# Own emission times for the last three groups, a direct last layer-2 product, and the first input in four loads

## The chip, the cores and the metric

The kernel runs on one core of one Trainium2 chip. The metric is the device time of one execution in microseconds (us). Every execution told of here was in the fast state, so nothing in this document compares runs of different states. The time of an execution is 1.7 to 2.9 us, mostly 1.8, longer than the span from the first to the last instruction; positions below are counted inside that span.

## The reference

Four graph layers work on 128 graphs of 128 nodes and 512 features, all in float32. They share one adjacency matrix `adj` of 128x128, and each is followed by a residual addition and a layer normalisation. Cut to what matters:

```python
x = ln(x + einsum('nm,bmd->bnd', adj, x) @ w0 + bias)                 # layer 0
q, k, v = x @ wq.T, x @ wk.T, x @ wv.T                                # layer 1
rel = adj.T * (q @ k^T);  rel = rel / norm(rel, axis=2)
x = ln(x + rel @ v)
h = x @ w2;  s1 = h @ a1;  s2 = h @ a2                                # layer 2
e = leaky_relu(s1[:, :, None] + s2[:, None, :]) * adj
x = ln(x + elu(softmax(e) @ h + beta * h))
A = adj @ x;  pre = A[:, :, None, :] + (C - A)[:, :, :, None]         # layer 3, C = A + b
x = ln(x + max(relu(pre), axis=-1))
```

## The kernel before

The graphs go through in 32 groups of four, numbered 0 to 31. Matrix products are done by TensorE, the rest by VectorE, ScalarE and GpSimd. Every operation is emitted with a time of its own. All are sorted by that time, and each engine then does its share strictly in the order that comes out; only the order matters, not the value of a time. One table serves all groups, each 28 steps behind the one before it, so that four groups in different layers overlap in the steady state:

```python
def emit(at, f, *args):
    pieces.append((at, lambda: f(*args)))
...
    # layer 2 of one group, t = 28 * g
    emit(t + 61.6, spread)          # p_s: s2 spread over the rows (TensorE)
    emit(t + 62.0, leaky)           # e (VectorE), then times adj (GpSimd)
    ...
    emit(t + 65.8, divide)          # softmax division of all four graphs (GpSimd)
    emit(t + 68.6, turn_att)        # p_eT: transposes
    each(t + 71.5, 1.0, gather)     # p_z, one graph each; ScalarE copies to zT
    left_factors(t + 75.3, s, "zT", "s_yz", f"z_{g}", 0)   # block sums s_z (GpSimd)
    product(t + 77, f"z_{g}", by_rows, s, "2", ...)        # r_z: seven block products
...
for g in range(NG):
    for layer in (layer0, layer1, layer2, layer3):
        layer(g, 28.0 * g)
for _, f in sorted(pieces, key=lambda p: p[0]):
    f()
```

The four large products of a group (called r_y, r_m, r_v and r_z in the profile) are done for four graphs together, in two by two blocks, with seven block products in place of eight. The price is sums of blocks: GpSimd makes four sums of the left factor (s_y, s_x, s_z), VectorE makes those of the weights once (t_m, t_v), and the results come out of PSUM through ScalarE copies and VectorE additions:

```python
def out(i):
    p, dst = r[REGION[i]], c(*BLOCK[i])
    if fresh and i in (1, 6, 5, 4):
        act.copy(dst, p)
    else:
        dve.tensor_tensor(dst, p, dst, ALU.add)
for n, i in enumerate(ORDER):
    emit(at + n, step, i)
    emit(at + n + 0.72, out, i)
```

The start loads the adjacency matrix and the first group's x as one megabyte on the SP queue, and w0, the bias, wk and w2 on the ScalarE queue. ScalarE then copies the transposed adjacency matrix `adjT` that the first product needs:

```python
def load(g):
    x1[g] = data.tile([P, G, D], FP, tag="x1", name=f"x1_{g}", bufs=3)
    nc.sync.dma_start(x1[g], x[g * G : (g + 1) * G].rearrange("b n d -> n b d"))
load(0)
nc.scalar.dma_start(w0_sb, w0.rearrange("(k p) f -> p k f", p=P))
nc.scalar.dma_start(bias_sb, on_all(bias0, D))
...
act.copy(adjT, pt[:, :P])
```

Names that come up again, in the order of a group's life: p_y (adjacency times x), r_y, p_xT (transposes), r_m (x times the product of wq and wk; tT is its result in SBUF), p_rel, r_v, p_o (attention output, then the residual x of layer 1), scr and d (the dot products for s1 and s2), p_s, e, p_eT, p_z, r_z, c (the layer-2 product), x3 (its residual), p_a (layer 3), mx and top (its maximum), st and mv (statistics).

## Time and profile before

| | before |
|---|---|
| time, median of 3 runs | 2324.65 us (2324.57 to 2328.68) |
| profiled span | 2324.9 us |
| TensorE busy | 2255.3 us, 97% |
| waits of TensorE in the first 130 us | 16.5 us |
| A: start of the last group's first r_m | 2187.26 us |
| from A to the end | 137.6 us |

TensorE is the bound in the middle. What can be had lies at the two ends, where no other group is there to fill the gaps. The lines for this are in the prediction. Later sections use one more stretch of the kernel before, the timeline of TensorE where it waits for the dot products d of group 0. The columns are start, us, engine, line, operation, output and inputs, sizes and count, then the idle time before it and what ended it:

```profile
118.91 0.62 PE L26 MATMUL p_s<-ident,d 128*128 128x128 f32 x4 [2.10 <-DVE d L26]
119.42 2.85 PE L26 MATMUL r_m<-xT,t_m 128*128 128x256 f32 x8
122.06 4.49 PE L26 MATMUL r_y<-w_sb,yT 128*128 128x256 f32 x16
```

After an idle time of 2.10 us, eight matmuls of r_m took 2.85 us and sixteen of r_y 4.49 us. Their usual times are 2.0 and 3.62.

### The profile page before, as it was taken

The numbers are of one execution on the slowest core, as the hardware profiler recorded it, in microseconds if no ns is written. First come the engines' busy times: TensorE is split into PE (matmuls) and PEld (weight loads), VectorE is DVE, ScalarE is ACT, GpSimd is POOL, SyncE is SP. The second block draws the span as 40 slices with busy tenths as digits, with TensorE's granted clock in tenths as the row PEclk, the third lists the DMA queues.
The fourth block names the chain that finished last, engine by engine and source line by source line (L and its number), as shares of the span: only waits on it lengthen the run. The fifth ranks groups of instructions, "written<-read, shape, count | busy, mean of one in ns | idle before, by whom it ended". The sixth has DMA issues, their size and how long they took to land.

```text
span 2324.9 us, 31209 instructions
## 1 busy us (share of the span) xinstructions
PE 2255.3 (97%) x11833; PEld 1922.6 (83%) x11833; DVE 1573.4 (68%) x3300; ACT 1007.8 (43%) x1804; POOL 960.9 (41%) x774
## 2 busy tenths in 40 slices
PE   7999999999999999999999999999999999999964
PEld 5888888888888888888888888888888888888753
DVE  3756776666776666776666776666776666777664
ACT  2224444444444444444445444444444444444434
POOL 3434444434444433444433444433444434444221
PEclk9999999999999999999999999999999999999987
DMA  4000011110011010011110011110011110010000
GB/s 159 19 16 9 32 37 37 37 37 10 28 37 37 37 37 14 24 37 37 37 37 19 19 37 37 37 37 19 19 37 37 37 37 19 19 37 19 19 18 36
DMA packets 38837, 75.20 MB, mean 32 GB/s; under 512 B 2976, under 2 KB 3104, under 8 KB 38688
## 3 DMA queue, kind: packets, MB, share of 16 engines
q1 hardware_dynamic: 36960, 69.81, 8.4%
q10 hardware_dynamic: 1728, 3.41, 0.4%
q8 instruction: 93, 1.52, 0.3%
q14 instruction: 56, 0.46, 0.1%
HBM read 39.65 MB, written 33.55 MB: 31 GB/s over the span
## 4 chain that ended last, share of the span: by engine, by line
PE 94%; DVE 3%; issue 1%; ACT 1%; POOL 1%; DMA 0%; POOLq 0%; ACTq 0%; SPq 0%; DVEq 0%
PE r_y L26 16%; PE r_v L26 16%; PE r_z L26 16%; PE r_m L26 16%; PE p_z L26 5%; PE p_a L26 5%; PE p_rel L26 5%; PE p_y L26 5%; PE p_o L26 5%; PE p_xT L26 2%; PE p_n L26 1%; DVE x L26 1%; DVE st L26 1%; PE p_eT L26 1%; PE p_m L26 1%
## 5 line engine op out<-in xcount | busy, mean ns | idle before, releaser
L26 ACT ACTIVATE x<-x,nmean,rstd 128x512 f32<-128x512 f32 x512 | 385.8, 808 | 134.3 <-DVE nmean L26 134.3
L26 DVE BATCH_NORM_STATS2 st<-x 128x6 f32<-128x512 f32 x512 | 352.5, 688 | 80.4 <-ACT x L26 71.7
L26 POOL TENSOR_TENSOR rstd<-ve,mhalf 128x4 f32<-128x4 f32 x128 | 141.8, 1108 | 258.2 <-DVE ve L26 255.1
L26 POOL TENSOR_TENSOR x<-x,bias_sb 128x512 f32<-128x512 f32 x128 | 175.3, 1371 | 136.5 <-PE p_y L26 136.5
L26 DVE SCALAR_TENSOR_TENSOR scr<-x,wa 128x512 f32<-128x512 f32 x256 | 212.7, 882 | 0.0
L26 ACT ACTIVATE x<-x,top 128x512 f32<-128x512 f32 x128 | 92.4, 722 | 265.5 <-DVE top L26 203.6
L26 DVE TENSOR_TENSOR x<-r_y,x 128x512 f32<-128x512 f32 x224 | 152.9, 683 | 59.1 <-PE r_y L26 56.0
L26 DVE TENSOR_TENSOR v<-r_v,v 128x512 f32<-128x512 f32 x96 | 65.9, 686 | 184.1 <-PE r_v L26 180.4
L26 POOL TENSOR_TENSOR s_x<-xT 128x512 f32<-128x512 f32 x64 | 81.9, 1279 | 235.8 <-ACT xT L26 235.8
L26 ACT COPY yT<-p_y 128x512 f32<-128x512 f32 x128 | 75.1, 587 | 219.9 <-PE p_y L26 219.9
L26 DVE SCALAR_TENSOR_TENSOR x<-p_o,rn,x 128x512 f32<-128x512 f32 x128 | 96.0, 750 | 101.3 <-PE p_o L26 98.3
L26 DVE SCALAR_TENSOR_TENSOR x<-m,x 128x512 f32<-128x512 f32 x128 | 113.7, 888 | 63.7 <-ACT m L26 52.7
L26 ACT COPY c<-r_z 128x512 f32<-128x512 f32 x128 | 74.9, 585 | 186.3 <-PE r_z L26 110.6
L26 PEld LDWEIGHTS p_y<-adjT,x 128*128 128x128 f32 x1024 | 136.7, 195 | 15.1 <-issue 8.7
L26 PE MATMUL p_a<-x,adjT 128*128 128x512 f32 x256 | 136.5, 618 | 13.0 <-ACT x L26 13.0
L26 PE MATMUL p_y<-adjT,x 128*128 128x128 f32 x1024 | 137.3, 279 | 8.5 <-DMA x<-in_x_dram 8.5
L26 PEld LDWEIGHTS p_z<-eT,x 128*128 128x128 f32 x1024 | 135.6, 193 | 8.5 <-issue 2.1
L26 PEld LDWEIGHTS p_rel<-tT,xT 128*128 128x128 f32 x1024 | 134.0, 192 | 6.5
L26 PE MATMUL p_z<-eT,x 128*128 128x128 f32 x1024 | 135.9, 276 | 0.0
L26 PE MATMUL p_rel<-tT,xT 128*128 128x128 f32 x1024 | 134.5, 275 | 0.0
L26 POOL TENSOR_TENSOR s_z<-zT 128x512 f32<-128x512 f32 x32 | 40.5, 1266 | 226.0 <-ACT zT L26 226.0
L26 PE MATMUL p_o<-v,rel 128*128 128x512 f32 x256 | 130.8, 593 | 0.0
(117 smaller groups left out, 5084.3 us busy)
## 6 DMA issues: line engine op xcount, KB each, us to landing
x<-in_x_dram SPq DMA_DIRECT2D x32, 1024.0 KB, 5.2
out_dram<-x SPq DMA_DIRECT2D x128, 256.0 KB, 2.0
w_sb<-in_L_gnn_weight_dram ACTq DMA_DIRECT2D x1, 1024.0 KB, 5.6
wq_sb<-in_L_gnn_Wq_dram SPq DMA_DIRECT2D x1, 1024.0 KB, 15.8
wk_sb<-in_L_gnn_Wk_dram ACTq DMA_DIRECT2D x1, 1024.0 KB, 12.2
wv_sb<-in_L_gnn_Wv_dram SPq DMA_DIRECT2D x1, 1024.0 KB, 18.9
w_sb<-in_L_gnn_W_dram ACTq DMA_DIRECT2D x1, 1024.0 KB, 17.1
a_sb<-in_L_gnn_a_dram SPq DMA_DIRECT2D x1, 512.0 KB, 16.1
```

What stands on the lines that cost most here:

```text
L26: return lambda *args, **kw: self.tc.keep_in_program_order(op(*args, **kw))
```

## The change

It has four parts.

1. The first group's x comes in four loads of 256 KB, one per graph, so that the first product can start on the first quarter. wk moves from the ScalarE queue to the SP queue.
2. Behind the product of wq and wk (p_m) the order is new: the transposes of wv come first, then the second group's four p_y. The four bias additions of the second group move ahead with its p_y.
3. The last three groups get rows of their own in the table, with times in units of one r step of 2.48 us, counted from A. The last group's normalisations of layers 2 and 3, its softmax division (there on VectorE in place of GpSimd) and its stores go graph by graph.
4. The last group's layer-2 product is done graph by graph, with four matmuls of 128x512 each, straight from w2. It needs no block sums, and it is read from PSUM without a copy. For this w2's block stays unchanged and its difference goes into a tile of its own.

The core of the diff, long parts cut:

```diff
+        if g == 0:
+            for b in range(G):
+                nc.sync.dma_start(x1[g][:, b, :], x[b])
+        else:
+            nc.sync.dma_start(x1[g], x[g * G : (g + 1) * G].rearrange("b n d -> n b d"))
...
-    nc.scalar.dma_start(wk_sb, wk.rearrange("(k p) f -> p k f", p=P))
+    nc.sync.dma_start(wk_sb, wk.rearrange("(k p) f -> p k f", p=P))
...
+    FIRST = {1: dict(y=row(-9.5, 0.3), bias=row(-9.2, 0.3))}
+    LAST = {
+        NG - 3: dict(exp=[0.8, 1.5, 2.2, 11.0], elu=[9.7, 12.3, 14.6, 17.2], ...),
+        NG - 2: dict(
+            scale=[5.6], apply1=row(24.3, 0.8), spread=[6.9], leaky=[7.4], ...
+            gather=row(36.7, 0.9), z_sums=row(39.95, 1.3),
+            z_w=[40.0, 41.8, 43.5, 45.2, 47.0, 49.4, 51.1], ...
+            elu=row(56.9, 2.3), norm2=[66.1], ...),
+        NG - 1: dict(
+            m=[0.0, 1.73, 3.46, 5.2, 7.4, 9.1, 10.8], scores=row(12.7, 0.9), ...
+            exps=row(53.2, 0.6), divide=row(53.9, 0.6), ...
+            gather=[55.2, 56.1, 60.5, 65.0], z_w=[57.0, 61.5, 66.0, 69.5], ...
+            store=[89.2, 91.0, 91.9, 92.8]),
+    }
...
+        def direct(b):
+            s["c", b] = psum.tile([P, D], FP, tag="r", name=f"c_{g}_{b}")
+            for k in range(K):
+                pe.matmul(s["c", b], s["zT"][:, k, b * P : (b + 1) * P],
+                          w2_sb[:, k, :], start=(k == 0), stop=(k == K - 1))
...
+        if g < NG - 1:
+            left_factors(t["z_sums"], s, "zT", "s_yz", f"z_{g}", 0)
+            product(t["z_w"], f"z_{g}", by_rows, s, "2", rows_of(lambda: s["c"]), True, begin)
+        else:
+            each(t["z_w"], direct)
...
-    each(26.0, 0.3, prepare_v)
+    each(row(18.0, 0.1), prepare_v)
```

## The prediction

> **What bounds the kernel now.** I read the page's busy times first, then the waits of TensorE, then the timeline of TensorE with its gaps, then ten-microsecond windows of the end.
>
> ```profile
> PE 2255.3 (97%) x11833; PEld 1922.6 (83%) x11833; DVE 1573.4 (68%) x3300; ACT 1007.8 (43%) x1804; POOL 960.9 (41%) x774
> ```
>
> TensorE is busy for 97% of 2324.9 us. The waits of TensorE between 140 and 2190 us are an empty list, so nothing but less matrix work could speed up the middle, and this change keeps that work. What can be had is 2324.9 - 2255.3 = 69.6 us of idle TensorE, plus matmuls that run at a lowered clock. The waits of TensorE in the first 130 us:
>
> ```profile
> PE p_y L26 <- DMA x<-in_x_dram: 8.5, 1, 8.5
> PE p_adjT L26 <- DMA adj_sb<-in_adj_dram: 3.3, 1, 3.3
> PE p_s L26 <- DVE d L26: 2.1, 1, 2.1
> PE r_m L26 <- DVE tT L26: 1.0, 1, 1.0
> PE p_xT L26 <- ACT x L26: 1.0, 1, 1.0
> PE r_y L26 <- POOL s_y L26: 0.6, 1, 0.6
> ```
>
> Columns: who waited for whom, us in total, times, longest. That is 16.5 us, half of it for x of the first group. The timeline of TensorE at the end (start, us, what, idle before it and its releaser):
>
> ```profile
> 2187.26 3.62 PE L26 MATMUL r_m<-xT,m_qk 128*128 128x256 f32 x16
> ...
> 2209.19 1.11 PE L26 MATMUL p_eT<-ident,e 128*128 128x128 f32 x4 [5.67 <-POOL e L26]
> 2210.10 3.22 PE L26 MATMUL r_v<-wvT,xT 128*128 128x256 f32 x8
> ...
> 2251.51 1.11 PE L26 MATMUL p_s<-ident,d 128*128 128x128 f32 x4 [4.42 <-DVE d L26]
> 2266.01 1.12 PE L26 MATMUL p_eT<-ident,e 128*128 128x128 f32 x4 [13.38 <-POOL e L26]
> ...
> 2304.78 5.46 PE L26 MATMUL p_a<-x,adjT 128*128 128x512 f32 x8 [12.15 <-ACT x L26]
> ```
>
> From the last group's first product (2187.26, called A) to the end there are 137.6 us. TensorE idles 5.67 + 4.42 + 13.38 + 12.15 us in four gaps, 2.7 us in three small ones, and about 14.7 us after its last matmul. There is no other group's work to fill the gaps, because all groups follow one table of times made for the steady state.
>
> **The Trainium skill.** "TensorE: Matmul & The Clock Gate", section "What's actually happening", says that the array's clock halves after an idle window of some 3.4 us and recovers after about as long a busy one. The trace agrees: r_v after the 5.67 us gap took 3.22 us, against 1.89 us elsewhere, and the granted clock of 2200 to 2210 us is 0.80. So each gap of two or more microseconds costs about 1.9 us more (0.5 on p_eT, 1.3 on r_v). "DMA: Bandwidth & Descriptors", section "Queues, rings and completion order", says that the SP and ACT queues share the same 16 engines and that completion is not first in, first out per issuing engine. The trace agrees as far as it goes: w0, issued at 0.74, landed at 6.3, and x, issued at 1.18 and as large, only at 12.06.
>
> **Part 1, first x in four loads.** PE needs the first quarter (256 KB), not all of x. In the trace the equally large bias load, issued at 1.23, landed at 8.5; I expect the first quarter by 7 to 8. But the ACT queue of the new kernel makes its third load (w2) wait for w0 (6.3 before), and in program order that load stands before ACT's table load and the copy adjT, which TensorE needs too. So adjT comes at 6.3 + 0.5 (issue) + 1.28 (table load) + 0.27 (copy) = 8.4, against 4.8. The first matmul moves from 12.2 to about 8.5: 3.7 us gained. It starts slow, 1.7 us per graph as before, and the remaining quarters (estimate: by 11.5) keep ahead. Everything up to the end of p_m at 45.34 was one chain behind it, with 0.63 us of gap, so it moves along to 41.6. wk now goes on the SP queue; it lands at about 18 (by bytes: 4.5 MB at the 345 GB/s that the first 22 us moved), before its use at 28.
>
> **Part 2, order behind p_m.** Now come the transposes of wv, then the second group's four p_y, then the four xT, then r_m alone. PE's work up to r_y of group 1 is unchanged: 1.74 + 3.5 + 1.74 + 7 x 1.73 = 19.1 us; before it took 22.3. In the new order p_y must wait for the bank that wvT frees, behind ACT's three x normalisations (2.12) and the copies 0.58 and 0.5: 1.3 us of idle, and the last copies of xT add a little. I get 20.6, a gain of 1.7. The wait of 2.1 for d stays, since VectorE is busy from 83 to 118 with the same list. Together the steady state starts 3.7 + 1.7 = 5.4 us earlier. Its 30 groups keep their order but for one instruction's operand (a weight block in a copy of its own).
>
> **Part 3, the end.** New positions count from A. One r step takes 1.73, p_a 0.86 per graph, p_z 0.87, p_rel 0.22 per matmul. VectorE takes 2.32 per graph of the x3 chain (x, x, st, mv), 1.6 per residual with st, 0.61 per scr, 0.92 per mx with top, 0.83 per st with mv. ACT takes 0.73 per 512-wide activation, POOL 1.27 per block sum and 1.0 per power. I laid these by hand along each engine's new order.
> - p_s of group 30 moves one step forward (6.9), so e is ready at 8.9, its exponentials at 14.5. TensorE has r_v 1 to do (17.0 to 18.8) while POOL divides (done at 17.1). The 5.67 gap and its slow clock go; p_rel waits about 1 us for tT, as ACT's exponentials now stand before that copy.
> - r_v with the p_a of group 29 ends at 33.8. Here VectorE and ACT lag: st of group 29's first graph waits for ACT (28.9 to 29.7), and ACT's copy of v comes at 36. The p_o and p_z share four PSUM banks, which the residuals free 1.6 us apart: p_o and p_z end at 44.7 instead of the table's 40, some 4 us lost.
> - r_z of group 30 waits once for POOL's sums (0.8), and runs to 58.2 with p_s of group 31 inside at 54.3. VectorE loses 1.5 us waiting for rstd. The 4.42 gap goes.
> - e of group 31: 55.1 to 56.4 on VectorE, 57.7 POOL, 58.5 the maximum, first exponential 59.7, division by graph on VectorE 60.1, p_z at 61.0. Of the 13.38 gap 2.8 is left, and the slow clock with it (1.9).
> - From 61.0: four p_z (3.5), 16 direct matmuls of 128x512 (13.9 by p_m, 1.8 more than the 12.1 of seven r_z), transposes 0.3, slow clock 1.9: c ends at 80.6. The old way would wait for sums and copies (0.70 and 1.06 in the trace), and needs all c before the first x3; that was the 12.15 gap.
> - VectorE becomes the bound: x3 of group 30 from 62 to 71, x3 of group 31 to 85.9, between them mx, then four st, mx, st by graph: 100.6 for the last nmean. One ACT apply 0.8 (four took 2.93), and from the last apply to the end 3.05 as before: 104.6.
>
> So the end falls from 137.6 to 104.6: 33.0 us. Sum 5.4 + 33.0 = 38.4; 2324.65 - 38.4 = 2286.
>
> **Rivals.** First, the table comes true: its last store stands at 92.8, with 0.8 and 3.05 behind it 96.7, 41 us gained at the end and 46 in all: 2278, just at 2%. For it: TensorE's work behind A is only about 77 us. Against it: VectorE's list alone takes 29.6 of the 37 us before p_z ends, and its in-order waits for ACT are not in the table. Second, VectorE's and ACT's order blocks more than I laid (each waits for the other in turn at p_a, mx, top, st, as the trace shows with 0.85 us before st each time), and two more gaps bring the slow clock: some 8 to 10 us lost, 2295. Third, w0 shares its bandwidth with the quarters of x and lands late, so adjT holds TensorE and the start gains only 1 to 2 us: 2289. Fourth, the start's gain is hidden because weights come late: wk at 18 against 28 speaks against it.
>
> **Range and chances.** The middle is fixed work, runs agree within 0.2% (2324.57 to 2328.68), and only about 85 us of known gaps can move. The start may be 2 us off, the hand-laid end 6 us: 2279 to 2294. More than 2% needs 2278.2 or less, which only the first rival gives: 0.09. Slower has nothing for it.
>
> **What would show it.** Right: p_y near 8.5 held by adjT rather than x; no gap above 2 us between A and A + 55; one gap of 2 to 4 us before p_z of the last group; VectorE busy almost without pause in the last 40 us; A to the end near 105. Wrong: A later than 2184, TensorE waiting longer than 2 us in the p_o and p_z stretch or for s_z, ACT rather than VectorE at the head of the last chain, or TensorE waits appearing in the steady groups.

## The result, and the profile after

| | before | after |
|---|---|---|
| time, median | 2326.66 us (4 runs, 2324.57 to 2328.75) | 2291.24 us (4 runs, 2290.3 to 2292.32) |
| profiled span | 2324.9 us | 2288.5 us |
| mean granted TensorE clock | 0.988 | 0.996 |
| first p_y starts | 12.20 | 8.45 |
| p_m starts | 31.60 | 27.40 |
| first r_y of group 1 starts | 67.65 | 64.26 |
| A | 2187.26 | 2182.83 |
| from A to the end | 137.6 | 105.7 |

The ratio of the times is 0.9848, with a 95% interval of 0.9831 to 0.9865. Ratios here are the mean time of one kernel's fast runs over that of the other's of the same rounds, so they are not quite the ratio of the medians quoted. The change is 1.5% faster, which is "within 2%". All outputs were correct.

The busy times of the kernel after:

```profile
PE 2250.7 (98%) x11809; PEld 1914.8 (84%) x11809; DVE 1577.0 (69%) x3319; ACT 1005.3 (44%) x1800; POOL 959.2 (42%) x775
```

TensorE's busy time fell by only 4.6 us. The other 31.8 of the 36.4 us by which the span fell were idle TensorE.

**The start.** These are the waits of TensorE in the first 130 us (who waited for whom, us in total, times, longest):

```profile
PE p_y L26 <- ACT adjT L26: 4.7, 1, 4.7
...
```

The wait of 8.5 us for x is gone. The first product now waits 4.7 us for adjT. Two new waits have come, 1.75 us for the block sums s_x and 1.52 for wvT, the transposed wv (both in the timeline below); a third, of 0.43 for x in r_y, comes after the wait for d. The waits for tT and for x in p_xT, 1.0 us each, are gone. The timeline of ScalarE says why adjT is late:

```profile
6.42 0.39 ACTq L114 DMA_DIRECT2D w_sb<-in_L_gnn_W_dram  x1
6.84 1.28 ACT L26 ACT_TABLE_LOAD   x1 [6.84 <-DMA w_sb<-in_L_gnn_weight_dram]
8.13 0.27 ACT L26 COPY adjT<-p_adjT 128x128 f32<-128x128 f32 x1
```

The third load of the ScalarE queue was held until w0 had landed, and the table load and the copy stand behind it. The hold came with the four loads. In one_load (below), where only these are undone, the same load goes out at 1.78 us and adjT is ready at 4.09. Why four loads bring it, no run shows. Behind p_m the timeline of TensorE and that of GpSimd read:

```profile
41.13 1.91 PE L26 MATMUL p_wv<-ident,wv_sb 128*128 128x128 f32 x16
44.56 3.84 PE L26 MATMUL p_y<-adjT,x 128*128 128x128 f32 x32 [1.52 <-ACT wvT L26]
...
50.05 3.72 PE L26 MATMUL r_m<-xT,m_qk 128*128 128x256 f32 x16
55.52 1.99 PE L26 MATMUL r_m<-s_x,t_m 128*128 128x256 f32 x8 [1.75 <-POOL s_x L26]
```
```profile
45.80 6.33 POOL L26 TENSOR_TENSOR x<-x,bias_sb 128x512 f32<-128x512 f32 x4 [13.00 <-PE p_y L26]
52.09 1.71 POOL L26 TENSOR_TENSOR s_x<-xT 128x512 f32<-128x512 f32 x1
```

GpSimd first did the four bias additions of the second group, for 6.33 us, and only then the sum that TensorE needed. And at the wait for d, which stood at 118.91 before:

```profile
115.51 0.62 PE L26 MATMUL p_s<-ident,d 128*128 128x128 f32 x4 [2.10 <-DVE d L26]
116.02 2.00 PE L26 MATMUL r_m<-xT,t_m 128*128 128x256 f32 x8
117.85 3.62 PE L26 MATMUL r_y<-w_sb,yT 128*128 128x256 f32 x16
```

The idle time is the same 2.10 us, but the matmuls behind it ran at full speed this time: 5.62 us in place of 7.34. That was luck, as shown below.

**The end.** The waits of TensorE from 2150 us on:

```profile
PE p_eT L26 <- DVE rs L26: 2.2, 2, 1.7
PE p_a L26 <- DVE mx L26: 1.8, 1, 1.8
PE p_a L26 <- ACT x L26: 1.7, 1, 1.7
...
```

Nothing is longer than 1.8 us; before, the list held 38.2 us, now it holds 10.2. The timeline of TensorE in the second half of that stretch:

```profile
2231.26 3.72 PE L26 MATMUL r_z<-t,s_z 128*128 128x256 f32 x16 [1.67 <-POOL s_z L26]
2236.10 1.97 PE L26 MATMUL r_z<-t,zT 128*128 128x256 f32 x8 [1.12 <-ACT c L26]
2237.91 0.65 PE L26 MATMUL p_s<-ident,d 128*128 128x128 f32 x4
...
2243.74 0.30 PE L26 MATMUL p_eT<-ident,e 128*128 128x128 f32 x1 [1.72 <-DVE rs L26]
...
2244.65 1.74 PE L26 MATMUL p_z<-eT,x 128*128 128x128 f32 x8
```

The first p_z took 1.74 us, in place of 1.05: the clock was down again, after idle times of 1.72 and 0.47 us. Beside the wait for s_z, the timeline of VectorE shows the dot products of the last group:

```profile
2229.40 0.68 DVE L26 SCALAR_TENSOR_TENSOR scr<-x,wa 128x512 f32<-128x512 f32 x1
...
2230.01 1.74 DVE L26 SCALAR_TENSOR_TENSOR scr<-x,wa 128x512 f32<-128x512 f32 x1
```

The same instruction on the same sizes took 0.68 us, and 1.74 us while GpSimd was making block sums. From 2246.93 to the end of its last instruction at 2283.66, the idle times that VectorE shows are 1.55, 0.17 and 0.65 us. So it is busy almost without pause; whether it alone sets the pace is tested below (x3_early).

### The profile page after: what moved, and what is told of

Its sections match the earlier page's. It is cut to its first block, busy times and chain, and to the rows that moved or that the text cites. A ratio compares the mean times of both kernels' runs of the same rounds, so it can differ in the third digit from the quotient of the medians.

```text
span 2288.5 us, 31182 instructions
## 1 busy us (share of the span) xinstructions
PE 2250.7 (98%) x11809; PEld 1914.8 (84%) x11809; DVE 1577.0 (69%) x3319; ACT 1005.3 (44%) x1800; POOL 959.2 (42%) x775
## 3 DMA queue, kind: packets, MB, share of 16 engines
q8 instruction: 93, 1.52, 0.3%
## 4 chain that ended last, share of the span: by engine, by line
PE 94%; DVE 4%; POOL 1%; ACT 1%; issue 1%; DMA 0%; ACTq 0%; DVEq 0%; POOLq 0%
PE r_y L26 17%; PE r_v L26 16%; PE r_m L26 16%; PE r_z L26 16%; PE p_z L26 5%; PE p_rel L26 5%; PE p_o L26 5%; PE p_a L26 5%; PE p_y L26 5%; PE p_xT L26 2%; DVE x L26 1%; PE p_n L26 1%; DVE st L26 1%; PE p_eT L26 1%; PE p_m L26 1%; PE p_s L26 1%
## 5 line engine op out<-in xcount | busy, mean ns | idle before, releaser
L26 POOL TENSOR_TENSOR rstd<-ve,mhalf 128x4 f32<-128x4 f32 (+1 forms) x134 | 144.5, 1078 | 245.3 <-DVE ve L26 241.3
## 6 DMA issues: line engine op xcount, KB each, us to landing
w_sb<-in_L_gnn_W_dram ACTq DMA_DIRECT2D x1, 1024.0 KB, 10.2
```

Of the source, the lines that this page charges most:

```text
L26: return lambda *args, **kw: self.tc.keep_in_program_order(op(*args, **kw))
```

## The experiments

All kernels gave correct results and all runs were fast. The edits are against the kernel after; the name of each run stands behind "Measured". "Before" is the median of the kernel before on the same chip in the same rounds. The kernel after was not run again, and the kernel before moved between 2326.58 and 2328.05 from batch to batch. So a difference from the 2291.24 of the kernel after compares medians of different rounds, and only the interval of start_only is clear of its interval (0.9831 to 0.9865). For differences of a few us positions in the traces are the better guide, but each trace is one execution.

### The start alone, and the end alone

The two halves of the change, each by itself:

```diff
# start_only
-    LAST = { ... }
+    LAST = {}
-        if g < NG - 1:
+        if g < NG:
# end_only
-        if g == 0:  (four loads)
+        nc.sync.dma_start(x1[g], x[g * G : (g + 1) * G].rearrange("b n d -> n b d"))
-    nc.sync.dma_start(wk_sb, ...)
+    nc.scalar.dma_start(wk_sb, ...)
-    FIRST = {1: dict(y=row(-9.5, 0.3), bias=row(-9.2, 0.3))}
+    FIRST = {}
-    each(row(18.0, 0.1), prepare_v)
+    each(row(26.0, 0.3), prepare_v)
```

Expected of the start alone:

> The new start (x in quarters, new order behind p_m) with the old table at the end, block sums for all groups. Theory 1 (start and end are separate stages, so their gains add): the last group's first r_m starts near 2182.8 as in the changed kernel, 4.4 us earlier than before (2187.3), the end stays 137.6 us long, the time is about 2322 (4 to 5 us under the kernel before). Rival (the start's gain is taken back later, hidden behind VectorE or a transfer): 2326, and the whole 35 us come from the end alone.

Measured (start_only): 2324.87 us (12 runs, 2321.93 to 2327.02) against 2326.61 before, a ratio of 0.999 (0.9981 to 0.9998). A came at 2182.92, which is 4.34 us earlier than before, and yet the end took 140.2 us from there. Its timeline of TensorE, at the gap that the kernel before shows at 2209.19:

```profile
2204.85 1.11 PE L26 MATMUL p_eT<-ident,e 128*128 128x128 f32 x4 [5.67 <-POOL e L26]
2205.76 3.62 PE L26 MATMUL r_v<-wvT,xT 128*128 128x256 f32 x8
...
2210.74 2.06 PE L26 MATMUL p_a<-x,adjT 128*128 128x512 f32 x2
2212.58 2.40 PE L26 MATMUL r_v<-wvT,xT 128*128 128x256 f32 x8
```

The gap is the same to a hundredth, but the lowered clock lasted longer. In the kernel before, the last three took 3.22, 1.10 and 1.89 us. From p_eT to the first p_z behind it there are 9.97 us here and 7.44 before: 2.5 of the 4.3 us won were given back. So the start's gain is there at A, and more than half of it is lost in the old end in this run. With one trace of each, this may be a draw of the clock as well. Neither expected number came: over its twelve runs the median is 1.7 us under the kernel before, between theory and rival.

Expected of the end alone:

> The old start with the new end. Theory 1 (the gains add): the last group's first r_m starts near 2187.3, from there to the end 105.7 us as in the changed kernel, time about 2295 (32 us under the kernel before). Rival: the end depends on where the start left VectorE and ACT, and the distance differs from 105.7 by more than 1 us.

Measured (end_only): 2293.69 us (4 runs, 2292.53 to 2293.93), a ratio of 0.9858 (0.9843 to 0.9873). A at 2187.23, as before, and 104.7 us to the end. That is 1.0 less than in the kernel after, just at the rival's border; the first p_z ran faster this time (1.17 us, 1.74 there). The end is worth 32.9 us by itself. With the 1.7 of the start alone that makes 34.6, close to the 35.4 of both.

### The first x in one load again

Only the four loads are undone; wk stays on the SP queue and the order stays new.

```diff
-        if g == 0:  (four loads)
+        nc.sync.dma_start(x1[g], x[g * G : (g + 1) * G].rearrange("b n d -> n b d"))
```

> The changed kernel with x of the first group in one load again. Theory (the quarters are what moved the first p_y from 12.2 to 8.45): the first p_y starts at 11 to 12.2, released by the DMA of x, and all later work is about 3 to 3.7 us later; time about 2294.5. Rival (moving wk behind wq on the SP queue did it, by leaving bandwidth to x): the first p_y stays at 8.5 to 9.5.

Measured (one_load): 2294.1 us (4 runs, 2291.47 to 2294.73), 2.9 us slower than the kernel after; ratio 0.9862 (0.9845 to 0.9878). TensorE again waited for x:

```profile
12.13 5.21 PE L26 MATMUL p_y<-adjT,x 128*128 128x128 f32 x32 [8.35 <-DMA x<-in_x_dram]
```

The quarters moved the first product, and moving wk did not. The profiled run was the fastest of its four. In it the gap before the last p_z was followed by matmuls at full speed, so its span of 2289.7 flatters it.

### The last layer-2 product with block sums again

The order of the end stays, with the last group's rows moved to suit the old product.

```diff
-            gather=[55.2, 56.1, 60.5, 65.0], z_w=[57.0, 61.5, 66.0, 69.5], ...
+            gather=[55.2, 56.2, 57.1, 58.0], z_sums=row(59.0, 1.3),
+            z_w=[59.3, 61.0, 62.7, 64.4, 66.2, 67.9, 69.6], ...
-        if g < NG - 1:
+        if g < NG:
```

> The changed kernel with the last group's layer 2 product in block sums again, its rows moved to follow the blocks. Theory A (the direct product pays because the first graph's c is ready 12 us earlier, though it is 1.8 us more of matmuls): the end is 2 to 6 us longer, 2293 to 2297. Theory B (VectorE is the bound behind c, and it has mx and st of group 30 to do while it waits for the blocks): within 1.5 us of the changed kernel, 2290 to 2293; then most of the 32 us is the order alone.

Measured (blocks_last): 2297.58 us (4 runs, 2296.41 to 2297.82), 6.3 us slower than the kernel after, its fastest run slower than the slowest of that kernel; ratio 0.9875 (0.986 to 0.989). From A to the end it took 111.5 us, 5.8 more. The layer-3 products p_a then wait three times for x from ScalarE, 6.7 us in all. Theory A holds, 0.6 us beyond its range. So some 6 us of the end's 32 belong to the direct product and the rest to the new order, as far as the one layout of rows tried here for the block sums goes.

### adjT copied by VectorE

If adjT is what holds the first product, a copy on an engine without that queue must free it.

```diff
-    act.copy(adjT, pt[:, :P])
+    dve.tensor_copy(adjT, pt[:, :P])
```

> The changed kernel with the copy adjT on VectorE, which is idle then, instead of ACT, whose third load waits for w0. Theory (adjT held the first p_y, the first quarter of x lands before 8): the first p_y starts at 6 to 7.5, released by the DMA of x, 1 to 2.4 us earlier, and the last group's first r_m moves with it. Rival (the quarters land only just in time): p_y at 8 or later, or p_y starts early but waits between graphs, and nothing is gained.

Measured (adjT_on_vector): 2290.15 us (4 runs, 2289.89 to 2291.25) against 2326.58 before; ratio 0.9842 (0.9827 to 0.9856). TensorE waited for x again:

```profile
7.59 5.97 PE L26 MATMUL p_y<-adjT,x 128*128 128x128 f32 x32 [3.77 <-DMA x<-in_x_dram]
```

The cause is right and the size smaller than I had expected: the first quarter lands at about 7.6, so adjT cost 0.86 us. But A did not move with it: it came at 2182.57, only 0.26 earlier. Up to 325 us the kernel is 0.77 ahead; between 328 and 340 us it loses 0.5 in steps too small for the list of waits. The same stretch loses 0.5 in combined and three_edits, which have this edit too. Why is not shown.

### The bias additions later

The second group's p_y stay early, and its bias additions go back to their old place.

```diff
-    FIRST = {1: dict(y=row(-9.5, 0.3), bias=row(-9.2, 0.3))}
+    FIRST = {1: dict(y=row(-9.5, 0.3))}
```

> The changed kernel with the second group's bias adds back at their old place, behind the block sums of xT in GpSimd's order. Theory (GpSimd did four bias adds first, 6.3 us, so that the third r_m waited 1.75 us for s_x): that wait is gone, r_y of group 1 starts 1.5 to 2 us earlier, at 62.3 to 62.8 instead of 64.26. Rival (GpSimd and VectorE slow each other, 1.27 to 1.7 us per operation, whatever the order): the wait shrinks by less than 0.7 us.

Measured (bias_late): 2288.84 us (4 runs, 2287.64 to 2289.66), 2.4 us under the kernel after by the medians; ratio 0.9835 (0.982 to 0.9849). The timelines of TensorE and of GpSimd:

```profile
50.98 3.72 PE L26 MATMUL r_m<-xT,m_qk 128*128 128x256 f32 x16
54.65 1.99 PE L26 MATMUL r_m<-s_x,t_m 128*128 128x256 f32 x8
```
```profile
51.99 1.26 POOL L26 TENSOR_TENSOR s_x<-xT 128x512 f32<-128x512 f32 x1 [18.25 <-ACT xT L26]
```

The wait for s_x is gone. From the start of p_m to the first r_y of group 1 it takes 35.05 us, against 36.86 in the kernel after and 36.05 in the kernel before. The theory of the wait holds: GpSimd's order cost 1.8 us in this stretch. Counted from p_m, the sums start 1.0 us earlier, and the first two, which r_m needs, take 2.6 in place of 3.4 us. VectorE was idle by then; its t_v, with no additions beside them, had taken 0.69 us each in place of 1.62 to 1.66.

The position that I expected was missed: r_y came at 63.38, not at 62.3 to 62.8, because p_m started 0.93 later in this run (28.33). A came at 2182.29, 0.54 earlier than in the kernel after. Nor do the 2.4 us of the medians belong to the edit alone: from A to the end this run took 104.0 us in place of 105.7, with the same instructions, and there the first two p_z took 1.06 us each, in place of 1.74 and 1.92.

### The old order behind p_m

```diff
-    FIRST = {1: dict(y=row(-9.5, 0.3), bias=row(-9.2, 0.3))}
+    FIRST = {}
-    each(row(18.0, 0.1), prepare_v)
+    each(row(26.0, 0.3), prepare_v)
```

> The changed kernel with the old order behind p_m (p_y of group 1 between the r_m, transposes of wv behind those of x). Measured in the two traces from the end of p_m to r_y of group 1: 22.3 us before, 23.1 after. Theory (the new order lost 0.8 us): r_y of group 1 starts at about 63.5 instead of 64.26. My prediction's step (the new order gains 1.7): at about 66. The steady state's clock after the wait of 2.1 us may shift the later stages by up to 1.8 us either way.

Measured (old_order_behind_p_m): 2290.34 us (4 runs, 2289.74 to 2290.88); ratio 0.9841 (0.9825 to 0.9858). From p_m to the first r_y of group 1: 36.05 us. As the change makes it, the new order costs 0.8 us. With the bias additions left where they were, it gains 1.0. The theory holds for this distance; r_y itself came at 64.00 instead of 63.5, because p_m started 0.55 later.

### Group 30's late parts earlier

VectorE does the x3 of group 30's graphs a little earlier in its order, to be done with them before the last group needs it.

```diff
-            elu=row(56.9, 2.3), norm2=[66.1], ...
+            elu=[55.8, 56.4, 59.2, 62.0], norm2=[65.0], ...
```

> The changed kernel with two graphs of group 30's x3 chain moved up into VectorE's waits of 1.10 and 1.55 us for the transposes of e of the last group. Theory (VectorE is the bound of the last 40 us): the end comes 2 to 2.7 us earlier, 2288.5 to 2289.3. Rival (TensorE's direct products set the pace, VectorE only follows): within 0.5 us of the changed kernel.

Measured (x3_early): 2291.22 us (4 runs, 2290.58 to 2291.36); ratio 0.9845 (0.983 to 0.9859). From A to the end 104.8 us, against 105.7 in the kernel after, with the first p_z slow in both (1.92 and 1.74 us). The last wait of p_a for mx fell from 1.75 to 0.82, but VectorE then waits 1.05 us for p_a, which stands behind c on TensorE. It also waits 0.82 us in two places for ScalarE's m. So of the 2.4 us filled, the end keeps 0.9, less than the theory's 2 and more than the rival's 0.5: TensorE's chain of p_z and c and VectorE's list are in step there, and VectorE alone is not the bound. The median did not move. In the profiled run A came at 2184.28, 1.45 later than in the kernel after, although the edit does not touch the start; the reason is the clock behind the wait for d (below).

### The powers later

Two small powers on GpSimd stand before block sums that r_z waits for. They were moved behind them, and with one of them the last activations and stores of group 29.

```diff
     NG - 3:
-            norm3=[42.0], apply3=row(44.0, 0.8), store=[47.4],
+            norm3=[45.0], apply3=row(48.5, 0.8), store=[51.5],
     NG - 1:
-            norm1=[40.65],
+            norm1=[44.9],
```

> The changed kernel with GpSimd's two powers for rstd (group 31's second norm, group 29's last) moved behind the four block sums of zT. Theory (in GpSimd's order they hold up the second and fourth sums, so that r_z waits 1.67 us for s_z, VectorE's nmean waits for a power and ACT's copy of c behind it costs 1.12 more): both waits of TensorE shrink to under 0.5 us each, p_eT of the last group starts 1 to 2.5 us earlier counted from the last group's first r_m (60.9 us in the changed kernel), the end as well, time 2289 to 2290.5. Rival (VectorE's eight scr, slowed to 1.7 us beside GpSimd, set the time of p_s and p_eT anyway): r_z waits less, but p_s waits instead and p_eT stays within 0.6 us of 60.9.

Measured (powers_late): 2292.12 us (4 runs, 2291.18 to 2292.93) against 2328.05 before; ratio 0.9847 (0.9833 to 0.986). The timeline of TensorE:

```profile
2229.96 3.72 PE L26 MATMUL r_z<-t,s_z 128*128 128x256 f32 x16 [0.24 <-POOL s_z L26]
...
2237.60 0.65 PE L26 MATMUL p_s<-ident,d 128*128 128x128 f32 x4 [2.20 <-DVE d L26]
2238.09 3.25 PE L26 MATMUL r_z<-w_sb,s_z 128*128 128x256 f32 x8
```

The wait for s_z fell from 1.67 to 0.24, and a wait of 2.20 for d came in its place, because d needs the power that now comes later. The r_z behind it ran at the lowered clock, and p_eT came at A + 63.1 in place of A + 60.9. The rival was right: the wait moved.

### The four edits together

The edits of the copy, the bias additions, x3 and the powers in one kernel, sent in one batch with the powers:

> The four edits together: adjT on VectorE, bias adds late, x3 early, powers late. If they add: 0.9 (first p_y at 7.6) + 1.8 (no wait for s_x) + 0.85 (x3) + 1 to 2 (powers) = 4.5 to 5.5 us under the changed kernel, about 2286; whether the slow clock falls after a short gap moves a single run by up to 2 us. If they overlap in the end (x3 and powers both only shift the same TensorE chain): 2288.

Measured (combined): 2291.19 us (5 runs, 2290.81 to 2293.81); ratio 0.9845 (0.9832 to 0.9859), no better than the kernel after. The first r_y of group 1 came at 61.63, 2.6 us earlier than in the kernel after, but A only 0.9 earlier. At the wait for d, whose length was again 2.09 us, the next line of TensorE's timeline reads:

```profile
113.72 3.61 PE L26 MATMUL r_m<-xT,t_m 128*128 128x256 f32 x8
```

That is 3.61 us for what took 2.00 in the kernel after, a loss of 1.6; 0.5 more went between 328 and 340 us, as with adjT on VectorE. From A to the end it took 107.3 us, because the edit of the powers makes the end worse.

### Three of them, and then a second group done directly

The edit of the powers is left out. In the second kernel group 30's layer-2 product is done graph by graph too.

```diff
# three_edits: adjT_on_vector + bias_late + x3_early
# last_two_direct: the same, and
-            gather=row(36.7, 0.9), z_sums=row(39.95, 1.3),
-            z_w=[40.0, 41.8, 43.5, 45.2, 47.0, 49.4, 51.1], exp=[51.5, 52.2, 56.2, 58.6],
-            elu=[55.8, 56.4, 59.2, 62.0],
+            gather=row(36.7, 0.9),
+            z_w=[40.0, 43.5, 47.0, 51.1], exp=[43.9, 50.5, 51.5, 56.2],
+            elu=[47.6, 55.8, 56.4, 59.2],
-        if g < NG - 1:
+        if g < NG - 2:
```

> The changed kernel with three edits that were each tried alone and each helped or did not hurt: the cast copy of the adjacency matrix on VectorE, no early bias add for the first group, group 30's late exp-linear parts a little earlier. Theory: the gains add where they lie on different waits. The last group's first r_m starts at about 2180.2 us of the span (2182.83 in the changed kernel, minus 0.3 for the copy, minus 0.5 for the bias adds, and x3_early's waits unchanged or better), the end takes 104 to 105.7 us from there, the profiled span is about 2285 and the median 2287 to 2288 (changed kernel 2291.2). Rival: each edit shifts the short gaps of TensorE against the slow-clock window, as in the combined kernel, and the sum is no better than the bias edit alone (2288.8) or even only the changed kernel's 2291.

Measured (three_edits): 2288.3 us (5 runs, 2287.97 to 2288.47) against 2327.81 before; ratio 0.9833 (0.9819 to 0.9846). A came at 2181.82 and the end took 104.9 us. The 2180.2 of my theory does not follow from its terms (2182.83 - 0.3 - 0.5 is 2182.0), and by these terms A came as laid. But the first r_y of group 1 came at 61.48, 2.8 us earlier than in the kernel after, and of this only 1.0 reached A. At the wait for d the eight r_m again took 3.59 us in place of 2.0, and 0.5 went between 328 and 340 us. So the rival is right for that part: in this run the clock took back much of what the start gave. The median is 2.9 us under the kernel after and level with the bias edit alone, whose interval overlaps.

> The three edits, and group 30's layer 2 product too is done graph by graph without block sums. Theory: the waits of r_z for GpSimd's block sums (1.67 us) and for ScalarE's block copy (1.12 us) are gone, VectorE's additions no longer run beside GpSimd's and take 0.7 us again in place of 1.7, while TensorE gets about 1.8 us more of matmuls: p_s of the last group comes at about 53.5 us after its first r_m in place of 55.1, p_eT at about 59.3 in place of 60.9, and the median is 1 to 3 us under that of the three edits. Rival: the four banks of group 30's product are freed late and hold up the last group's, or TensorE's longer work eats what the waits gave: within 1 us of the three edits, or slower.

Measured (last_two_direct): 2286.21 us (4 runs, 2285.94 to 2286.68) in the same rounds; ratio 0.9824 (0.9811 to 0.9837). No run of it is as slow as the fastest of the three edits. Its timeline of TensorE:

```profile
2224.69 10.46 PE L26 MATMUL c<-w_sb,zT 128*128 128x512 f32 x24
2234.99 0.60 PE L26 MATMUL p_s<-ident,d 128*128 128x128 f32 x4
```

The theory holds. The two waits are gone, each of the eight scr takes 0.69 us where two took 1.74 and 1.75, p_s comes at A + 53.45 (I had said 53.5) and p_eT at A + 58.9 (59.3), and from A to the end it takes 102.7 us. It is the best kernel of this study: 2.1 us under the three edits in the same rounds, 5.0 us under the kernel after (other rounds) and 1.8% under the kernel before.

## Why the prediction was right or wrong

The prediction was right: the change is within 2%, and the measured 2291.24 lies in the range of 2279 to 2294. Its point was 5.2 us too low. Of this, 2.0 us is the base. I subtracted from 2324.65, the median of three runs, while a fourth run moved it to 2326.66; the traced execution, from which the gains were worked out, took 2326.87. The other 3.0 us is the gain, 38.4 predicted and 35.4 measured. In the profiled pair the gain was 36.4 (4.4 at the start and 32.0 at the end); the profiled run of the kernel after was the fastest of its four.

**Part 1 was right.** The step "the first matmul moves from 12.2 to about 8.5" measured 8.45, held by adjT through the wait of the ScalarE queue for w0, as it said, and the experiment with the copy on VectorE shows that cause. One_load shows that the quarters are what did it. At p_m the gain had grown to 4.20, since the slow first stretch of p_y took 5.77 in place of 6.58 us and a wait for s_y grew by 0.36. The length of that slow stretch is luck too: in the four other kernels with the same start (named below) it was 5.38 to 6.21 us. The landing of wk came true (18 predicted, 18.5 measured), but not by its sum: 4.5 MB at 345 GB/s make 13 us, and the trace moved 331 GB/s in those 22 us.

**Part 2 was wrong.** The step that failed is "I get 20.6, a gain of 1.7". The stretch took 23.13 us, from 41.13 to 64.26, against 22.31 before: a loss of 0.8. The wait for wvT that it named was there (1.52 us, estimated 1.3). What it left out was GpSimd. The change moves four bias additions ahead, they stood before the sums s_x, and TensorE waited 1.75 us. The two engines also slowed each other. I counted 1.27 us for an operation of GpSimd, but those four took 1.58 each while VectorE was making t_v, whose operations took 1.62 to 1.66 us in place of 0.69; and the first two sums then took 1.71 and 1.59 beside VectorE's late work. The Trainium skill states the reason in "SBUF — State Buffer", section "Who interferes with whom": a VectorE instruction with two SBUF inputs contends with a GpSimd instruction that reads SBUF, because its second input comes through the interface that the two engines share. The trace agrees: scr, with x and wa from SBUF, took 0.68 us alone and 1.74 beside block sums, and 0.69 throughout once those sums were gone. I had not used that page. That the order itself is good and only the additions were misplaced is shown by the bias edit (35.05 against 36.05 us of the old order).

**A gain that no step had, and it was luck.** From the first r_y of group 1 to A the kernel after was 1.0 us quicker than the kernel before, though it does the same work. The matmuls behind the wait for d ran at full speed, 1.7 us less, and a new wait of 0.43 for x behind them took back 0.6 with its restart. So the start gave 4.43, not 5.4: +4.20 at p_m, -0.81 in part 2 and +1.0 here. This +1.0 is not the change's. The start is the same in start_only, blocks_last, x3_early and powers_late. Behind the same gap the eight r_m took 1.99 us in start_only and powers_late, but 3.16 in blocks_last and 3.10 in x3_early:

```profile
116.15 1.08 PE L26 MATMUL p_s<-ident,d 128*128 128x128 f32 x4 [2.10 <-DVE d L26]
117.03 3.10 PE L26 MATMUL r_m<-xT,t_m 128*128 128x256 f32 x8
```

A came at 2182.92 and 2182.95 in the first two, at 2184.39 and 2184.28 in the others. So in five traces the start is worth 2.9 to 4.4 us, and the kernel after had the best of them. The prediction's rule "each gap of two or more microseconds costs about 1.9 us more" holds in some executions and not in others.

**Part 3 was right in its course and 1.1 us off in its end** (a gain of 33.0 predicted, 32.0 measured). Positions are counted from A:

| step of the prediction | predicted | measured |
|---|---|---|
| p_rel waits for tT | 1 | 0.62 |
| r_v with the p_a of group 29 ends | 33.8 | 35.1 |
| p_o and p_z end | 44.7 | 43.1 |
| r_z waits for s_z | 0.8 | 1.67 |
| p_s of group 31 | 54.3 | 55.1 |
| p_z of group 31 starts | 61.0 | 61.8 |
| c of group 31 ends | 80.6 | 81.0 |
| last nmean of VectorE starts | 100.6 | 100.7 |
| end | 104.6 | 105.7 |

The last nmean came on time, so the whole 1.1 us lies behind it: ScalarE's last apply ended 1.3 us after it in place of 0.8, and from there to the end it took 3.55 us in place of 3.05. That it came on time is partly luck, as two steps missed in opposite directions. "The p_o and p_z share four PSUM banks, which the residuals free 1.6 us apart ... some 4 us lost" was wrong. The residuals came 1.6 to 2.4 us apart, but only the second p_z waited for one (0.42 us); the last two did not. I had assumed a strict rotation of the banks, and the trace shows that the product did not wait so. "r_z of group 30 waits once for POOL's sums (0.8)" was too small. It waited 1.67 for s_z and then 1.12 for a ScalarE copy of c, which I had not foreseen. The last experiment takes both waits and the slowed dot products away and moves p_s from A + 55.1 to A + 53.45. So these together were on the path; powers_late, which removes one wait alone, only moved it to d. The gap before p_z came as 1.72 and 0.47 us, 2.2 in place of 2.8, with the slow clock behind it. That clock varies as well: with the same instructions behind A, the distance to the end was 104.7 us in end_only, 103.5 in one_load, 105.6 in adjT_on_vector, 104.0 in bias_late and 105.0 in old_order_behind_p_m. In the two shortest the first two p_z took 1.06 us each, in the two longest (kernel after and adjT_on_vector) 1.74 to 1.92. So the predicted 104.6 lies inside what one set of instructions shows. "VectorE becomes the bound" is half right: it shows only 2.37 us of idle time in its last 37 us, but x3_early filled 2.4 us of its waits and gained only 0.9.

**The rivals.** The first, a table that comes true at 96.7 us, did not happen, and even the best kernel needed 102.7. The second, orders that block and bring the slow clock, did not happen in the change; powers_late shows what it looks like, with the wait of 2.20 us for d and r_z at 3.25 us behind it. The third and fourth, a hidden start, are refuted for the mechanism they named; but in start_only something else hid most of the start's gain, the longer slow clock behind the 5.67 us gap.

What stays open is why the clock comes back sooner in one execution and later in another of the same instructions. The freely running window that the last section names would fit, but this is only argued: no run here sets its phase on purpose.

## What to carry to other kernels

In a pipeline that is full in the middle, give the first and the last groups an order of their own: the last three groups were worth 32 us here (about 6 of them by the direct product), and the middle nothing. When an operation is moved ahead, lay out the queue of every engine that it brings along, the quiet ones too; four harmless additions on GpSimd cost 1.8 us of TensorE. In the last groups, where nothing fills the waits, a product with more matmuls and no sums can be the shorter one, and a gain of one or two microseconds is better read from positions in the trace than from medians. Even a position is one draw: behind the same gap of 2.1 us the same eight r_m took 1.99 us in one trace and 3.16 in another. So compare several traces of a stretch before a gain there is put down to an edit.

## What the Trainium skill lacked or had wrong

- "TensorE: Matmul & The Clock Gate" ("What's actually happening") gives an idle window of about 3.4 us before the clock drops. Here gaps of 2.1 us, and of 1.7 plus 0.5, were enough in some runs: eight r_m behind the same 2.1 us gap took 2.00 us in the kernel after, 2.85 before, 3.59 and 3.61 in three_edits and combined. It does say that the window runs freely. A rule for a single gap shorter than the window, which cost from nothing to 1.7 us here, is missing. Nor is the recovery the same each time: behind the same 5.67 us gap, the stretch from p_eT to the next p_z took 7.44 us in the kernel before and 9.97 in start_only.
- "SBUF — State Buffer" ("Who interferes with whom") has the contention of VectorE and GpSimd right. It calls the shared ports an exclusive lock and gives the loss of one engine at a time. It does not say what two streams that run side by side for long cost each other: here VectorE went from 0.68 to 1.74 us and GpSimd's sums from 1.27 to 1.72, so both pay.
- "DMA: Bandwidth & Descriptors" ("Queues, rings and completion order") says that a DMA engine takes turns between the queues that have work. Two loads of 1 MB on two queues, issued 0.44 us apart, landed at 6.3 us (w0) and 12.06 us (x) in the kernel before. With turns taken one would expect them to land close together; why they did not, no run here shows.
